# Triangle steps of three batches in a new order, and a residual that the accumulator takes over

## The chip, the cores and the metric

The kernel runs on one core of a Trainium2 chip. The metric is the device time of one execution in microseconds (us), lower being better. A core has five engines with a queue each: TensorE (PE in the profile, its weight loads PEld), VectorE (DVE), ScalarE (ACT), GpSimd (POOL), and SyncE (SP), which here issues most of the DMA transfers. Each engine works its queue off in order.

## The reference, cut to what matters

The input x is 4 batches of 64 x 64 tokens with 256 channels, all in float32. Layer 0 is self-attention over the 4096 tokens of a batch with a residual. Layer 1 is a triangle attention over the 64 x 64 grid, with 8 heads of 32 channels, followed by two layer norms and an MLP:

```python
scores = jnp.einsum('bilhd,bljhd->biljh', q, k) / np.sqrt(d_k)
att = jax.nn.softmax(scores, axis=2)
out = jnp.einsum('biljh,bilhd,bljhd->bijhd', att, v1, v2)
attn_out = out.reshape(B, N, N, E) @ Wo
h = x_in + attn_out
h = _layer_norm(h, ln_agg_g, ln_agg_b)
mlp = jax.nn.relu(h @ W1 + b1) @ W2 + b2
h = mlp + h
return _layer_norm(h, ln_out_g, ln_out_b)
```

The addition `mlp + h` is the "second residual" of this document. The triple product over att, v1 and v2 is the heavy part of layer 1: the kernel multiplies att by v2 elementwise, and then sums over l with v1 as weights on TensorE.

## The kernel before, in words

The order of all work is written out by hand (a manual schedule): the order of calls in the Python code is the order in each engine's queue. Tiles come from pools of a fixed number of buffers by tag, so a new tile waits until the last readers of the tile that had the buffer are done.

For each of the four batches, `layer0` runs the attention of layer 0 and the projections q, k, v1, v2 of layer 1, and then `run_layer1` runs 32 triangle steps: four pairs of heads (`pair`) by eight groups of eight rows i (`ig`). In the triangle stages of batches 1 to 3, the token work of the batch before (output projection, both layer norms and the MLP) is woven in, one tile of 256 tokens for every two steps. The tokens of batch 3 remain for the end; its first tile still goes with the triangle stage, and `alone` does the other 15 by themselves.

One triangle step has eight products, numbered by m. `product` multiplies a [128, 64] piece of att by v2 into a [128, 2048] tile: products of list `D_` run on VectorE (L799, tile R, three buffers, reading att from PSUM), those of list `Q_` on GpSimd (L799, tile Rp, two buffers, reading the copy attP in SBUF[...]). `npool` gives GpSimd three products in even steps and two in odd ones of batches 1 to 3, so VectorE has five and six. `accumulate` (L808) multiplies a finished product on TensorE by the selector weights wsel that hold v1, in four column tiles of 32, and sums into acc; each step has two acc tiles in PSUM, and `take` (L816) copies each by ScalarE into ao, which `store` (L823) writes to memory. Between these stand the preparations of the next step: `sums` (row sums, L731, and reciprocals, L733, on VectorE), `weights` (es, L741, eight ScalarE passes), `turn` (transposes into att on TensorE, L753, and the ScalarE copy attP, L758), and `stationary` (wsel, L777, ScalarE). In the first three pairs a quarter of the next pair's scores (`scores`, sp, L704, TensorE) and its exponentials (`take_scores`, S, L714, ScalarE) goes with every two steps.

The token tile's own steps are methods of `Tokens`: `heads` (L863, L868: output projection and residual x into PSUM tile hp), `stats_a` (bn_stats of hp on VectorE), `roots` (L893, L895: logarithm and exponential on ScalarE for the inverse root), `polish` (L902 to L910: seven small operations that refine it, on GpSimd in the stage and on VectorE in `alone`), `affine_a` (L915: normed h, ScalarE), `turn` (L933 transposes into htp, and L936: hT with the norm's gain and shift), `residue` (L945, L946: z = h times gain plus shift and b2, GpSimd), `hidden` (L956) with `rectify` (L963), `outputs` (L974: second MLP product into zp), `stats_o` (L887: z = zp + z on VectorE, then bn_stats), `affine_o` (L915), and `finish` (L982, L983: gain and shift of the last norm, GpSimd, then the output transfer). The PSUM tiles hp, htp, mp and zp share two buffers.

In the code before, `run_layer1` spreads these over two steps: in the even step heads, stats_a, outputs, stats_o and roots; in the odd step polish, affine_a, affine_o, turn, residue, finish, hidden and rectify. Each accumulation follows its product closely, and scores stand before the last accumulations of the even steps.

Of the kernel before, what the change touches and what calls it, by code (L numbers as in the profile page):

```python
# [33 lines left out]
def attention_then_triangle_kernel(  # L34
# [96 lines left out]
    def add_b2():  # L131
        b2_bc = work.tile([P, C], F32, tag="st", name="b2_bc", bufs=3)
        nc.gpsimd.dma_start(out=b2_bc, in_=b2.partition_broadcast(P))
        nc.gpsimd.tensor_tensor(lb2_bc, lb2_bc, b2_bc, ALU.add)

    lag_sb = column(lag, 2, "lag_sb")
    lab_sb = column(lab, 2, "lab_sb")
    b1_sb = column(b1, 4, "b1_sb")
# [218 lines left out]
    def layer0(b, F, safe, rest):  # L357
# [278 lines left out]
        if old:  # L636
            rest.turn(t0)
            rest.load(t0 + 1)
            rest.residue(t0)
# [12 lines left out]
        proj(last, "v2", 1, None, stage[2][:, 1, :], nc.scalar)  # L652
        return L
# [5 lines left out]
    class Layer1:  # L659
        def __init__(self, b, io, safe):  # L660
            self.b, self.io, self.safe = b, io, safe

            self.aT = dram.tile([C, 2, N // 2, N], F32, tag="aT", name="aT")
            io["a"] = self.aT
            self.S, self.v2, self.qk, self.v1, self.att, self.ao = {}, {}, {}, {}, {}, {}

# [116 lines left out]
        def begin(self, step):  # L783
            self.R, self.begun = {}, set()
            self.acc = [None, None]
            self.ao[step] = work.tile([P, 4, 8, N], F32, tag="k8", name="ao")

        def product(self, step, m):
            n, h = divmod(m, 2)
            att, attP = self.att[step]  # L790
            k = self.npool(step)
            if m >= 8 - k:
                R = work.tile([P, D, N], F32, tag="Rp", name="Rp")
                eng, src = nc.gpsimd, attP[:, m - 8 + k, :]
            else:
                R = work.tile([P, D, N], F32, tag="R", name="R", bufs=3)
                eng, src = nc.vector, att[:, n, ts(h, 64)]
            v2 = self.v2[step // NIG]
            eng.tensor_tensor(R, src.unsqueeze(1).to_broadcast([P, D, N]), v2[:, h], ALU.mult)  # L799
            self.R[m] = R  # L800

        def accumulate(self, step, m):
            n, h = divmod(m, 2)
            if self.acc[n // 2] is None:
                self.acc[n // 2] = pa("acc")
            acc, w, R = self.acc[n // 2], wsel[step % 2], self.R.pop(m)
            for c in range(4):
                nc.tensor.matmul(  # L808
                    acc[32 * c : 32 * c + 32, n % 2, :], w[:, n, c, 16 * h : 16 * h + 32],
                    R[:, ts(c, 8), :].rearrange("p d j -> p (d j)"),  # L810
                    start=n not in self.begun, stop=n in self.begun,
                )
            self.begun.add(n)

        def take(self, step, np, acc):
            nc.scalar.copy(self.ao[step][:, ts(np, 2)].rearrange("p k d j -> p k (d j)"), acc)  # L816
# [14 lines left out]
    class Tokens:  # L831
        def __init__(self):
            self.ios = []
            self.A = {}
            self.h, self.hT, self.hid, self.z, self.zp, self.hps = {}, {}, {}, {}, {}, {}
            self.mv = self.rs = None
# [48 lines left out]
        def stats_o(self, tt):  # L885
            z = self.z[tt]
            nc.vector.tensor_tensor(z, self.zp.pop(tt), z, ALU.add)  # L887
            self.stats(z, 2)
# [31 lines left out]
        def affine_a(self, tt):  # L920
            self.h[tt] = work.tile([P, 2, C], F32, tag="h", name="h", bufs=1)
            self.affine(self.h[tt], self.hps.pop(tt), 0)

        def affine_o(self, tt):
            self.affine(self.z[tt], self.z[tt], 2)


        def turn(self, tt):
            h = self.h[tt]
            tp = pb("htp").rearrange("p (c t) -> p c t", c=2)  # L930
            for cc in range(2):
                for n in range(2):
                    nc.tensor.transpose(tp[:, cc, ts(n, P)], h[:, n, ts(cc, P)], ident)  # L933
            hT = work.tile([P, 2, 256], F32, tag="hT", name="hT")
            for cc in range(2):
                nc.scalar.activation(  # L936
                    hT[:, cc, :], tp[:, cc, :], AF.Identity, bias=lab_sb[:, cc : cc + 1], scale=lag_sb[:, cc : cc + 1]
                )
            self.hT[tt] = hT


        def residue(self, tt):
            h = self.h.pop(tt)
            z = self.z[tt] = work.tile([P, 2, C], F32, tag="s4", name="z")
            nc.gpsimd.tensor_tensor(z, h, lag_bc.unsqueeze(1).to_broadcast([P, 2, C]), ALU.mult)  # L945
            nc.gpsimd.tensor_tensor(z, z, lb2_bc.unsqueeze(1).to_broadcast([P, 2, C]), ALU.add)  # L946
# [20 lines left out]
        def outputs(self, tt, n, apart=None):  # L967
            if n == 0:
                self.zp[tt] = pb("zp").rearrange("p (n c) -> p n c", n=2)
            zp = self.zp[tt]  # L970
            if apart is not None:
                zp = self.zp[tt + 1] = apart("zp").rearrange("p (n c) -> p n c", n=2)
            for fc in range(4):
                nc.tensor.matmul(  # L974
                    zp[:, n, :], self.hid[tt][:, fc, ts(n, P)], w2_sb[:, fc, :],
                    start=(fc == 0), stop=(fc == 3),
                )

# [9 lines left out]
        def alone(self, t0, t1):  # L988
# [5 lines left out]

            self.stats_a(t0 + 1)
            normed(0, 2)
            self.affine_a(t0 + 1)
            for tt in range(t0, t1 - 1):
# [6 lines left out]
                self.turn(tt + 1)  # L1005
                self.residue(tt + 1)
                if tt + 2 < t1:
                    normed(0, 2)
                    self.affine_a(tt + 2)
                for n in range(2):  # L1010
                    self.outputs(tt, n)
# [12 lines left out]
            for n in range(2):  # L1024
                V.tensor_tensor(z[:, n], self.zp[tt + n][:, n], z[:, n], ALU.add)
                self.stats(z, 2, (n,))
                normed(2 + n, 3 + n)
# [4 lines left out]


# [3 lines left out]
    def run_layer1(b, L, rest, ahead, F):  # L1037
        old = b > 0
        t0 = NP * (b - 1)

        t1 = NP * b + (b == NB - 1)
        if b == 0:
            ahead.load(0)
        waiting = behind = None
        for step in range(NSTEP):
            pair, ig = divmod(step, NIG)
            more = step + 1 < NSTEP

            now = t0 + step // 2
            nxt = now + 1  # L1050
            even, odd = old and step % 2 == 0, old and step % 2 == 1
            even_a, odd_a = even and nxt < t1, odd and nxt < t1

            forward = step // 4 * 3 + step % 4 if b == 0 and step % 4 < 3 else None
            L.begin(step)
            if F is not None:
                ahead.fetch(F, b + 1, step)
# [3 lines left out]
            L.fetch_v1(step + 2)  # L1061
            if scored:
                L.take_scores()
            if waiting is not None:
                L.take(step - 1, 1, waiting)
                L.store(step - 1)
            if step == 2:
                L.fetch_v2(1)
            if ig == 0 and 0 < pair < NPAIR - 1:
                L.fetch_v2(pair + 1)  # L1070
# [12 lines left out]
            if odd:  # L1083
                rest.polish(0 if odd_a else 2, 4, nc.gpsimd)
            if even_a:
                rest.heads(nxt, 0)
# [7 lines left out]
            if odd_a:  # L1094
                rest.affine_a(nxt)
            if odd:
                rest.affine_o(now)
            if even_a:
                rest.heads(nxt, 1)
                rest.load(nxt + 1)  # L1100
# [10 lines left out]
            if even:  # L1111
                rest.outputs(now, 0)
            L.product(step, D_[2])
            L.accumulate(step, D_[2])
            if odd_a:
                rest.turn(nxt)
# [3 lines left out]
            if even_a:  # L1120
                rest.stats_a(nxt)
            if late:
                next_weights()
            if even:
                rest.outputs(now, 1)
            if k == 3:
                L.product(step, Q_[2])
            if odd_a:
                rest.residue(nxt)
            if odd:  # L1130
                rest.finish(now)
            if odd_a:
                mps = [rest.hidden(nxt, 0), rest.hidden(nxt, 1)]
            L.product(step, D_[3])
            L.accumulate(step, D_[3])
            L.take(step, 0, L.acc[0])
# [3 lines left out]
            if odd_a:  # L1140
                rest.rectify(nxt, 0, mps[0])
                rest.rectify(nxt, 1, mps[1])
# [4 lines left out]
            if odd_a:  # L1147
                mps = [rest.hidden(nxt, 2), rest.hidden(nxt, 3)]
                rest.rectify(nxt, 2, mps[0])
                rest.rectify(nxt, 3, mps[1])  # L1150
# [9 lines left out]
            if even:  # L1160
                rest.stats_o(now)
                rest.roots(0 if even_a else 2, 4)
            if b == NB - 1 and step in (28, 29, 30):
                rest.load(t1 + step - 27, True)
            waiting = L.acc[1]
        if F is not None:
            ahead.fetch(F, b + 1, NSTEP)
        L.take(NSTEP - 1, 1, waiting)
        L.store(NSTEP - 1)

    def run(safe):
        rest, ahead = Tokens(), Ahead()
        with tc.manual_schedule():
            F = front0(0)
            for b in range(NB):
# [5 lines left out]
                run_layer1(b, L, rest, ahead, F)  # L1181
                if F is not None:
                    rest.ios.append(L.io)
            for n in range(2):
                rest.heads(NP * (NB - 1) + 1, n, psum=pc)
# [51 lines left out]
```

## Time and profile before

| what | before |
|---|---|
| time, median of 3 (range) | 3936.88 us (3935.04 to 3937.64) |
| span of the profiled execution | 3936.3 us |
| granted TensorE clock, mean | 0.994 of full speed |
| busy share PE, DVE, ACT, POOL | 95%, 69%, 46%, 49% |
| triangle stages of batches 1, 2, 3: first product to the next stage | 1373.7 to 1865.6, 2318.3 to 2811.5, 3264.1 to about 3762 us |
| lone token tiles | about 3762 to the end |

A line of a group reads: source line, engine, operation, output<-input by the program's tile names, shapes and count, then busy us in total and mean ns of one, then the engine's idle time ahead of it and what ended most of that. In a timeline a line reads: start, duration, engine, source line, operation, count of merged instructions, and in brackets the idle time of the engine ahead of it and its releaser. A matrix product in float32 appears as two instructions, so one `accumulate` (four column tiles) appears as x8. Triangle steps in pairs are called a cycle: it repeats 16 times in each stage.

### The profile page before, as it was taken

The numbers are of one execution on the slowest core, as the hardware profiler recorded it, in microseconds if no ns is written. First come the engines' busy times: TensorE is split into PE (matmuls) and PEld (weight loads), VectorE is DVE, ScalarE is ACT, GpSimd is POOL, SyncE is SP. The second block draws the span as 40 slices with busy tenths as digits, with TensorE's granted clock in tenths as the row PEclk, the third lists the DMA queues.
The fourth block names the chain that finished last, engine by engine and source line by source line (L and its number), as shares of the span: only waits on it lengthen the run. The fifth ranks groups of instructions, "written<-read, shape, count | busy, mean of one in ns | idle before, by whom it ended". The sixth has DMA issues, their size and how long they took to land.

```text
span 3936.3 us, 59354 instructions
## 1 busy us (share of the span) xinstructions
PE 3737.0 (95%) x23302; PEld 1742.6 (44%) x23302; DVE 2708.9 (69%) x2291; ACT 1814.4 (46%) x3775; POOL 1927.0 (49%) x1024
## 2 busy tenths in 40 slices
PE   9999998889999999998999999999899999999998
PEld 5444444433444444443344454444344444444376
DVE  4454499896444499998454459999644447999965
ACT  3333455554333455554333345555433335555544
POOL 4000098993000099998000049999500007999954
PEclk9999999999999999999999999999999999999999
DMA  4111445552111434323111154233211134331221
GB/s 119 50 51 48 116 139 137 136 144 96 49 51 51 121 74 91 84 53 87 52 51 46 54 131 93 55 85 74 75 48 47 49 99 103 84 85 45 53 70 50
DMA packets 439713, 309.38 MB, mean 79 GB/s; under 512 B 299328, under 2 KB 404544, under 8 KB 432128
## 3 DMA queue, kind: packets, MB, share of 16 engines
q1 hardware_dynamic: 419952, 291.12, 28.2%
q10 hardware_dynamic: 16240, 8.59, 0.8%
q0 software_dynamic: 3232, 5.78, 0.6%
q8 instruction: 186, 3.05, 0.3%
q14 instruction: 103, 0.84, 0.1%
HBM read 165.88 MB, written 139.46 MB: 78 GB/s over the span
## 4 chain that ended last, share of the span: by engine, by line
PE 72%; ACT 9%; DVE 6%; DMA 5%; POOL 3%; issue 3%; SPq 3%; ACTq 0%; POOLq 0%; DVEq 0%
PE o L432 24%; PE acc L808 12%; PE proj L489 8%; PE s L410 7%; PE mp L956 5%; PE zp L974 3%; DVE R L799 3%; PE sp L704 3%; PE v1p L514 3%; POOL Rp L799 2%; ACT S L714 2%; ACT ao L816 2%; SPq L823 2%; PE hp L863 2%; PE y L474 1%
## 5 line engine op out<-in xcount | busy, mean ns | idle before, releaser
L799 POOL TENSOR_TENSOR Rp<-attP,v 128x2048 f32<-128x2048 f32 x328 | 1490.1, 4569 | 449.9 <-DMA qk<-k 324.7
L799 DVE TENSOR_TENSOR R<-att,v 128x2048 f32<-128x2048 f32 x696 | 1547.3, 2273 | 95.4 <-PE acc L808 44.2
L439 DVE TENSOR_TENSOR esum<-esum,e 128x2048 f32<-128x2048 f32 x224 | 512.7, 2289 | 583.4 <-ACT e L421 580.5
L808 PE MATMUL acc<-R,wsel 128*32 128x512 f32 x5568 | 727.7, 605 | 64.3 <-DVE R L799 43.1
L421 ACT ACTIVATE e<-s 128x1024 f32<-128x1024 f32 x512 | 496.5, 1021 | 403.6 <-PE s L410 381.8
L902 POOL TENSOR_SCALAR nt<-mv 128x4 f32<-128x4 f32 (+1 forms) x51 | 9.9, 193 | 1283.6 <-DVE mv L880 1279.5
L816 ACT COPY ao<-acc 128x1024 f32<-128x1024 f32 x256 | 261.5, 1021 | 547.2 <-PE acc L808 436.2
L432 PE MATMUL o<-e,vlo 128*128 128x512 f32 x1024 | 473.7, 605 | 0.0
L432 PE MATMUL o<-e,vhi 128*128 128x512 f32 x1024 | 472.6, 605 | 0.0
L808 PE MATMUL acc<-Rp,wsel 128*32 128x512 f32 x2624 | 350.7, 610 | 35.1 <-POOL Rp L799 34.9
L808 PEld LDWEIGHTS acc<-R,wsel 128*32 128x32 f32 x5568 | 143.2, 109 | 396.0 <-issue 198.7
L432 PEld LDWEIGHTS o<-e,vlo 128*128 128x128 f32 x1024 | 184.0, 189 | 280.8 <-issue 280.8
L432 PEld LDWEIGHTS o<-e,vhi 128*128 128x128 f32 x1024 | 184.3, 189 | 279.7 <-issue 279.7
L410 PE MATMUL s<-gT,fT 32*128 32x512 f32 x2048 | 302.2, 640 | 4.8 <-ACT e L421 4.5
L956 PE MATMUL mp<-hT,w 128*128 128x256 f32 x1024 | 250.4, 390 | 39.6 <-ACT hT L936 39.6
L741 ACT ACTIVATE es<-S,rd 128x64 f32<-128x64 f32 x1024 | 258.4, 338 | 26.9 <-DVE rd L733 25.0
L451 DVE RECIPROCAL rec<-den 128x512 f32<-128x512 f32 x32 | 107.4, 3357 | 215.6 <-PE den L449 215.6
L974 PE MATMUL zp<-w,hid 128*128 128x256 f32 x1024 | 247.3, 387 | 2.9 <-ACT hid L963 2.9
L956 PEld LDWEIGHTS mp<-hT,w 128*128 128x128 f32 x1024 | 182.9, 189 | 117.4 <-ACT hT L936 57.8
L974 PEld LDWEIGHTS zp<-w,hid 128*128 128x128 f32 x1024 | 186.5, 191 | 67.5 <-issue 40.3
L501 ACT COPY st<-proj 128x512 f32<-128x512 f32 x104 | 60.9, 585 | 293.2 <-issue 165.9
L410 PEld LDWEIGHTS s<-gT,fT 32*128 32x128 f32 x2048 | 82.9, 182 | 193.7 <-issue 172.6
(153 smaller groups left out, 3795.3 us busy)
## 6 DMA issues: line engine op xcount, KB each, us to landing
v<-v2d SPq DMA_DIRECT2D x24, 1024.0 KB, 13.0
v1c<-v1d SPq DMA_DIRECT2D x128, 128.0 KB, 3.0
aT<-ao SPq DMA_DIRECT2D x1024, 16.0 KB, 1.9
A<-aT SPq DMA_DIRECT2D x256, 64.0 KB, 2.1
out_dram<-z SPq DMA_DIRECT2D x63, 256.0 KB, 2.2
y<-yT SPq DMA_DIRECT2D x56, 256.0 KB, 2.0
q<-st SPq DMA_DIRECT2D x56, 256.0 KB, 2.6
v1d<-st SPq DMA_DIRECT2D x56, 256.0 KB, 2.2
```

What stands on the lines that cost most here:

```text
L410: nc.tensor.matmul(s_ps[r // 2][:, r % 2, :], fT[rows, tt, ts(n, P)], gT[rows, ts(qb, QB)], start=True, stop=not safe,)
L421: nc.scalar.activation(e[g][:, 2 * j : 2 * j + 2, :], s_ps[j], AF.Exp)
L432: nc.tensor.matmul(o_ps[qb], F.v[tt][:, r * 4 + n, :], es[:, r, :], start=(k == 0 and r == 0), stop=(k == 7 and r == 3),)
L439: nc.vector.tensor_tensor(esum[qb], esum[qb], es, ALU.add)
L489: nc.tensor.matmul(ps, w[:, cc, rows], y(qb, cc), start=(cc == 0), stop=(cc == 1))
L514: nc.tensor.matmul(ps[:, ts(n, C)], y(qb, cc)[:, ts(m * 2 + n, P)], wv1_sb[:, cc, :], start=(cc == 0), stop=(cc == 1),)
L741: nc.scalar.mul(self.e[:, i, :], rows[:, i, :], rec[:, i : i + 1])
L799: eng.tensor_tensor(R, src.unsqueeze(1).to_broadcast([P, D, N]), v2[:, h], ALU.mult)
L808: nc.tensor.matmul(acc[32 * c : 32 * c + 32, n % 2, :], w[:, n, c, 16 * h : 16 * h + 32], R[:, ts(c, 8), :].rearrange("p d j -> p (d j)"), ...
L816: nc.scalar.copy(self.ao[step][:, ts(np, 2)].rearrange("p k d j -> p k (d j)"), acc)
L956: nc.tensor.matmul(self.mp[:, fc % 2, :], w1_sb[:, cc, ts(fc, P)], self.hT[tt][:, cc, :], start=(cc == 0), stop=(cc == 1),)
L974: nc.tensor.matmul(zp[:, n, :], self.hid[tt][:, fc, ts(n, P)], w2_sb[:, fc, :], start=(fc == 0), stop=(fc == 3),)
```

## The change

Three things are changed for batches 1 to 3, and the stage of batch 0 keeps the old order (`first_layer1`).

1. *New order.* `next_layer1` starts each step with the first product on GpSimd and on VectorE, and then closes the step before (its last two accumulations, the copy of its second acc, the store): the end of one step lies in the next. Accumulations stand in groups of two or three. The even step has outputs, stats_a, stats_o, roots, polish, affine_a, affine_o and turn; the odd step has hidden, rectify, finish and the heads of the tile after the next. Scores follow a table `due` and stand at the step's end. The aim is that fewer waits fall between products and accumulations.
2. *Second residual on TensorE.* `residue` and the addition in `stats_o` go for these tiles. `carried` makes a second copy of the turned h with gain, shift and b2 (hT2, ScalarE), and `outputs` adds its transposes into the accumulator zp. The statistics and `affine_o` read zp directly.
3. *Lone tiles.* h alternates between tags "h" and "A", z between "s4" and "es"; for the first tile outputs come ahead of turn; the two halves of the last tile are both summed before the first is closed. The lone tiles keep `residue`.

In `layer0`'s end the heads of the second tile are computed as well, and the next tile is loaded.

```diff
@@ Layer1, Tokens
-        def take(self, step, np, acc):
-            nc.scalar.copy(self.ao[step][:, ts(np, 2)].rearrange("p k d j -> p k (d j)"), acc)
+        def take(self, step, np):
+            nc.scalar.copy(
+                self.ao[step][:, ts(np, 2)].rearrange("p k d j -> p k (d j)"), self.acc[step][np]
+            )
...
         def stats_o(self, tt):
-            z = self.z[tt]
-            nc.vector.tensor_tensor(z, self.zp.pop(tt), z, ALU.add)
-            self.stats(z, 2)
+            z = self.z.get(tt)
+            if z is not None:
+                nc.vector.tensor_tensor(z, self.zp.pop(tt), z, ALU.add)
+            self.stats(self.zp[tt] if z is None else z, 2)
...
-        def affine_a(self, tt):
-            self.h[tt] = work.tile([P, 2, C], F32, tag="h", name="h", bufs=1)
+        def affine_a(self, tt, far=False):
+            tag = "A" if far and tt % 2 else "h"
+            self.h[tt] = work.tile([P, 2, C], F32, tag=tag, name="h", bufs=1)
...
+        def carried(self, tt):
+            self.h.pop(tt)
+            self.hT2[tt] = self.turned(lab2_sb, tag="s4")
...
                 nc.tensor.matmul(
                     zp[:, n, :], self.hid[tt][:, fc, ts(n, P)], w2_sb[:, fc, :],
-                    start=(fc == 0), stop=(fc == 3),
-                )
+                    start=(fc == 0), stop=(fc == 3 and tt not in self.hT2),
+                )
+            if tt in self.hT2:
+                for cc in range(2):
+                    nc.tensor.matmul(
+                        zp[:, n, ts(cc, P)], self.hT2[tt][:, cc, ts(n, P)], ident,
+                        start=False, stop=(cc == 1), is_transpose=True,
+                    )
...
@@ next_layer1, which takes the place of run_layer1 for batches 1 to 3
+            product(Q_[0])
+            product(D_[0])
+            if step > 0:
+                close(step - 1)
...
+            if step % 2 == 0:
+                for n in range(2):
+                    rest.outputs(now, n)
+                if more:
+                    L.stationary(step + 1)
+                if first:
+                    rest.stats_a(nxt)
+                product(D_[1])
+                if more:
+                    L.sums(step + 1)
+                    L.weights(step + 1)
+                add(D_[0], D_[1], Q_[0])
+                product(Q_[1])
+                if more:
+                    L.turn(step + 1)
+                product(D_[2])
+                add(D_[2], Q_[1])
+                rest.stats_o(now)
+                k0 = 0 if first else 2
+                rest.roots(k0, 4)
+                rest.polish(k0, 4, nc.gpsimd)
+                product(Q_[2])
+                product(D_[3])
+                if first:
+                    rest.affine_a(nxt)
+                rest.affine_o(now)
+                if first:
+                    rest.turn(nxt)
+                add(D_[3])
+                L.take(step, 0)
+                if first:
+                    rest.normed(nxt)
+                    rest.carried(nxt)
+                product(D_[4])
+                pend = [D_[4], Q_[2]]
...
+            else:
...
+                    mps = [rest.hidden(nxt, fc) for fc in range(2)]
...
+                add(D_[0], D_[1])
...
+                    mps = [rest.hidden(nxt, fc) for fc in range(2, 4)]
...
+                add(Q_[0], D_[2])
+                if more:
+                    L.turn(step + 1)
+                product(D_[3])
+                rest.finish(now)
+                add(D_[3], Q_[1])
+                L.take(step, 0)
+                product(D_[4])
...
+                        rest.heads(aft, n)
...
+            if step in due:
+                L.scores(*due[step])
+            if step % 2 == 1:
+                product(D_[5])
+                pend = [D_[4], D_[5]]
```

## The prediction

> **What bounds the kernel now.** I read the page's busy times first, then the stretches of 50 us, then the timeline and the chain of waits inside one two-step cycle, then the lone token tiles at the end. From the page (engine, busy us and share; then groups with count, busy, mean ns):
>
> ```profile
> PE 3737.0 (95%) x23302; PEld 1742.6 (44%) x23302; DVE 2708.9 (69%) x2291; ACT 1814.4 (46%) x3775; POOL 1927.0 (49%) x1024
> ...
> L799 POOL TENSOR_TENSOR Rp<-attP,v 128x2048 f32<-128x2048 f32 x328 | 1490.1, 4569 | 449.9 <-DMA qk<-k 324.7
> L799 DVE TENSOR_TENSOR R<-att,v 128x2048 f32<-128x2048 f32 x696 | 1547.3, 2273 | 95.4 <-PE acc L808 44.2
> ```
>
> The shares are averages over stages, so the busy times by stretch (PE, PEld, DVE, ACT, POOL), one inside a changed triangle stage and one in the lone tiles:
>
> ```profile
> 1550.00:1600.00 50.00, 47.16 (x367) 22.73 (x360) 46.96 (x39) 28.14 (x76) 47.99 (x25) 1.00 0.16 40
> ...
> 3850.00:3900.00 50.00, 48.40 (x234) 40.52 (x233) 31.76 (x109) 24.10 (x67) 25.36 (x20) 1.00 0.21 59
> ```
>
> In the triangle stage three engines are 94 to 96% busy: no engine can be relieved alone. What sets the cycle is in the chain of waits there (start, us, what):
>
> ```profile
> 1572.40 1.04 PE acc L808 x8
> ...
> 1573.51 1.02 ACT ao L816
> ...
> 1574.58 2.03 PE sp L704 x64
> ...
> 1576.63 2.05 ACT S L714 x2
> 1578.67 0.86 ACT ao L816
> 1579.53 1.90 ACT es L741 x8
> ...
> 1582.35 1.02 ACT h L915 x2
> ```
>
> TensorE stands still three times in it (before sp, after sp, before mp) because ScalarE's queue does the copies one after another. The cycle closes at 31.0 us: starts of the output's last pass (L983) are 31.0, 31.0, 31.0, 30.1 us apart. The durations that I use are in the timeline:
>
> ```profile
> 1567.10 0.66 PE L753 MATMUL att<-ident,es 128*128 128x128 f32 x4
> ...
> 1567.85 0.27 ACT L758 COPY attP<-att 128x128 f32<-128x128 f32 x1 [2.20 <-PE att L753]
> ...
> 1574.55 0.30 ACT L893 ACTIVATE ln<-mv,eps 128x4 f32<-128x4 f32 x1
> ...
> 1574.88 0.20 ACT L895 ACTIVATE rs<-ln 128x4 f32<-128x4 f32 x1
> ...
> 1579.39 0.20 POOL L903 TENSOR_TENSOR nt<-rs 128x4 f32<-128x4 f32 x1
> ...
> 1581.03 4.56 POOL L799 TENSOR_TENSOR Rp<-attP,v 128x2048 f32<-128x2048 f32 x1
> ```
>
> At the end, one lone tile takes 10.2 us, by this loop through POOL and an output DMA:
>
> ```profile
> 3902.91 1.27 POOL L983 TENSOR_TENSOR z<-z,lob_bc 128x512 f32<-128x512 f32 x1
> ...
> 3906.47 1.26 POOL L945 TENSOR_TENSOR z<-h,lag_bc 128x512 f32<-128x512 f32 x1 [2.30 <-DMA out_dram<-z]
> ...
> 3907.77 1.02 ACT L915 ACTIVATE h<-hp,rn 128x256 f32<-128x256 f32 x2 [4.96 <-DVE nt L902]
> 3908.39 1.00 PE L933 MATMUL htp<-ident,h 128*128 128x128 f32 x4 [1.74 <-ACT h L915]
> ```
>
> h waits until L945 has read the only h buffer, and L945 waits until z's buffer has been written out.
>
> **What the Trainium skill says.** "TensorEngine Tiling (Array Packing)", Key Properties: changing the tiling mode drains TensorE. The trace agrees: a group of accumulations takes 0.88 us inside a run and 0.97 to 1.00 where an untiled matmul follows (accumulations start at 1587.02 and 1587.91, the next matmul at 1588.88), so grouping is worth about 0.1 us for each run saved. "Perfetto Trace Analysis", Identifying the Most-Contended Engine: matmul busy time is no measure of TensorE's headroom; so I sum block starts instead. "SBUF — State Buffer", Who interferes with whom: a VectorE op with two SBUF inputs and a GpSimd op lock each other out. In the lone tiles L904 takes 1.15 us beside L983 and 0.16 without it; in the triangle stage products read PSUM and show no such thing.
>
> **The change, part by part.** A cycle is two steps; even step E has vector products D0 to D4 and POOL products Q5 to Q7, odd step O has D0 to D5 and Q6, Q7.
>
> *Work removed.* The second residual leaves POOL (L945, L946: 2 x 1.28 = 2.6 us a cycle) and VectorE (L887: 0.69). VectorE falls to 11 x 2.21 + 4 x 0.55 (bn) + 2 x 0.83 (sums) = 28.2 us a cycle, POOL to 5 x 4.55 + 1.9 (polish) + 2.6 (finish) = 27.2.
>
> *Work added.* ScalarE makes a second pair of 128x256 passes (hT2, 2 x 0.51 us, from the hT row); it is 56% busy, and they stand behind hT and ahead of the second acc copy, which waits for Q7 anyway: nothing. TensorE gets four transposes into zp, 4 x 0.11 = 0.44 (the yc transposes).
>
> *Order.* The score matmuls move to the odd step's end, behind the two heads (2.27 us), in which ScalarE copies the accumulator away: both waits around sp go. But the number of accumulation runs stays at eight a cycle, so grouping itself brings nothing. And the statistics move: stats, roots, polish and h now follow one another within one even step, and POOL's third product Q7 stands behind the polish. Queue orders of the changed kernel: ScalarE has attP ahead of Ln; POOL has polish ahead of Q7; TensorE has Q7's accumulation ahead of everything of the odd step. That is a closed loop. Its part off TensorE, from the start of att: attP starts 0.72 later (0.70 to 0.75), Ln 0.20 after it, rs 0.33 and 0.20 long, POOL 0.04 + 1.65 (1579.39 to 1581.03), product 4.55, 0.05 to TensorE: 7.74 us. TensorE's own part from Q7's accumulation to the next att: 0.97; mp 1.92; two acc 1.86; mp 1.92; two acc 1.86; att 0.59; two acc 1.86; heads 2.27; sp 1.93; two acc 1.86; zp 1.92 + 1.73 + 0.44 = 4.09; three acc 2.73; sum 23.86. Cycle 31.60 us with scores, 29.67 without. TensorE uses 4.3 of the 7.74 (D2, Q6, htp, D3, D4) and idles 3.4: first for h, then for Q7. Queued behind that wait are the hidden matmuls, and through them the whole odd step. VectorE, 28.2, and POOL, 27.2, fit inside; with three R buffers VectorE is ahead at each of its accumulations, and es is ready 0.5 us before att's turn (acc copy 1.02, S 2.05, wsel 0.99, es 2.02 after the closing accumulations).
>
> *Stage sum.* Eleven cycles have scores, then three without, then two without heads or hidden, where VectorE sets 28.4 and 27.5. With 1.45 from the first product to the cycle's origin and 1.86 to close: 1.45 + 347.6 + 89.0 + 55.9 + 1.86 = 495.8. In the first cycle the third product waits for the DMA of v2d out of a stage tile, as before (until 1383.9), and now the statistics stand behind it: 2.5 us more, 498.3. Before: 1373.7 to 1865.6 = 491.9 and 2318.3 to 2811.5 = 493.2. So +6.4 and +5.1. In batch 3 all five late cycles have heads and hidden: 1.45 + 347.6 + 148.4 + 1.86 = 499.3, and the same DMA wait ended later (3277.3): 5.6 us; 504.9 against 3264.1 to 3762.0 plus 2.3 for two heads that move in, 500.2: +4.7. Together +16.2. The hT2 passes in the end of layer 0, where TensorE waits for ScalarE at times: +1 for all.
>
> *Lone tiles.* h alternates between two buffers, z between two tags: the POOL loop goes, and TensorE's own 2.17 + 0.43 + 3.46 + 3.45 = 9.5 us is left. 14 x 0.65 = 9.1 less. Outputs ahead of the first turn save about 1.3, the earlier h in the tile before the last 1.3, closing the last two halves together about 1 (VectorE's polish of one no longer waits for the other's multiply). Together -12.7.
>
> Sum: +16.2 + 1 - 12.7 = +4.5 us: 3936.9 + 4.5, about 3941 us.
>
> **Rivals.** *Slower:* the loop has more in it than I count. If es misses its 0.5 us, or each handover costs 0.1 more (7 of them), 33 scored cycles gain 0.5 and 15 others 0.3: +21, about 3962. For it: every such error goes one way, a queue cannot be earlier than its chain. Against it: in the kernel before, the chain of 31.0 us has no unexplained gap over 0.04. *Faster, a little:* my att-to-attP or block starts are 0.3 to 0.4 us a cycle too long (a modelled end, a drain counted twice), and the lone tiles bring 15: 48 x 0.35 + 2 = -19 against the forecast, about 3922. *Faster, much:* the loop does not bind because Q7's accumulation or the roots come earlier than the queues say; then TensorE's 28.2 and VectorE's 28.2 bind, some 28.8 a cycle against 30.8: 48 x 2 + 12.7 = -109, 3828. The saturated three engines speak for it as the aim; the three queue orders speak against it.
>
> **How the numbers follow.** Forecast 0.40 (3929 to 3945, within 0.2%), slower 0.35, a little faster 0.20, much faster 0.05. Range 3912 to 3970: it leaves out the much faster case, and the ends of the two near ones.
>
> **What would show it.** Right: in the triangle stage L983 starts about 31.6 us apart and 29.7 in the last cycles; TensorE idles some 2 us before htp (released by h) and 1 us before an acc of Rp (released by POOL L799 after the polish); sp starts without a wait for ao; lone tiles 9.5 us apart. Wrong: a cycle under 30.5 with scores (the loop is not closed), one over 32.2 (a second wait, then look at es and S on ScalarE), or lone tiles still at 10.2.

## The result: slower, and the profile after

| what | before | changed |
|---|---|---|
| time, median (range) of 4 runs each | 3935.96 us (3933.39 to 3937.64) | 3980.37 us (3975.71 to 3981.99) |
| ratio to before, with its interval | | 1.0111 [1.0094, 1.0129] |
| span of the profiled execution, granted TensorE clock | 3936.3 us, 0.994 | 3973.9 us, 0.987 |

The change costs 1.1%; 3941 us was forecast. The page of the changed kernel, with engines' busy times and the two product rows (columns as before):

```profile
PE 3749.0 (94%) x23498; PEld 1782.4 (45%) x23498; DVE 2703.7 (68%) x2242; ACT 1857.9 (47%) x3873; POOL 1803.1 (45%) x928
...
L807 DVE TENSOR_TENSOR R<-att,v 128x2048 f32<-128x2048 f32 x696 | 1558.9, 2275 | 190.0 <-PE acc L817 153.0
L807 POOL TENSOR_TENSOR Rp<-attP,v 128x2048 f32<-128x2048 f32 x328 | 1487.7, 4568 | 424.0 <-ACT attP L766 386.9
```

GpSimd has lost 124 us of work (1927.0 to 1803.1), the removed residual, and the products' mean times have not moved. But VectorE's idle time ahead of its products has doubled (95.4 to 190.0), most of it until accumulations release its R buffers, and GpSimd now waits for attP. The stretches of the changed kernel (columns PE, PEld, DVE, ACT, POOL, clock, DMA) answer to the two shown before:

```profile
1550.00:1600.00 50.00, 45.43 (x364) 21.52 (x362) 44.64 (x39) 31.10 (x82) 39.80 (x25) 0.97 0.14 33
3850.00:3900.00 50.00, 47.02 (x233) 40.33 (x232) 38.39 (x115) 26.26 (x70) 23.34 (x20) 1.00 0.28 78
```

In the triangle stage no engine is saturated any more: TensorE fell from 47.16 to 45.43, VectorE from 46.96 to 44.64, GpSimd from 47.99 to 39.80. Each now waits for another, which is what a closed chain looks like. Here it is, from the chain of waits of the changed kernel (start, us, what):

```profile
1651.26 0.60 PE att L761 x4
...
1651.94 0.27 ACT attP L766
1652.20 0.21 ACT ln L905
...
1652.43 0.21 ACT rs L907
...
1654.17 0.23 POOL rn L922
1654.40 4.52 POOL Rp L807
...
1658.96 1.06 PE acc L817 x8
1660.03 1.92 PE mp L985 x8
```

From the start of att to the accumulation of Q7 it takes 7.70 us. TensorE fills part of that and waits twice; its waits from 1500 to 1700 us (us in total, times, longest):

```profile
PE htp L950 <- ACT h L927: 11.0, 6, 2.0
PE acc L817 <- POOL Rp L807: 3.8, 4, 1.0
```

For the lengths of the cycles I take the starts of the last pass of the output (L1018; before L983), in batch 1 the first eleven intervals, and then the three without scores:

| kernel | intervals, us | without scores, us |
|---|---|---|
| before | 31.9, 31.0, 31.0, 30.1, 31.1, 31.0, 31.0, 30.1, 31.1, 31.0, 31.0 | 30.1, 30.9, 30.1 |
| changed | 34.9, 31.7, 31.7, 32.2, 31.7, 31.7, 32.3, 31.7, 31.8, 32.2, 31.7 | 30.5, 29.8, 29.8 |

Where the 37.6 us between the two spans lie: the three triangle stages 11.2, 8.9 and 8.8 (503.1, 502.1 and 509.0 us against 491.9, 493.2 and 500.2, the last with the 2.3 of the two heads that moved in), batch 0's stage 6.0 (439.0 against 433.0), the stretches of layer 0 0.9 (the first) and 1.4 (the other three), and the lone tiles 0.5 (172.5 against 172.0). These sum to 37.7 by their rounded values. The profiled execution of the changed kernel is its shortest, 3975.71, and the median lies 4.7 above it.

The lone tiles should have become shorter and did not: their last passes (L1018) are mostly 10.3 us apart, those of before 10.2. Timeline of the changed kernel in one of them, GpSimd, VectorE, ScalarE and TensorE (start, duration, and so on; in brackets the idle time ahead and its releaser):

```profile
3878.80 1.27 POOL L1018 TENSOR_TENSOR z<-z,lob_bc 128x512 f32<-128x512 f32 x1
...
3878.94 1.15 DVE L916 TENSOR_TENSOR nt<-nt 128x2 f32<-128x2 f32 x1
3880.03 1.27 POOL L974 TENSOR_TENSOR z<-h,lag_bc 128x512 f32<-128x512 f32 x1
...
3880.12 1.20 DVE L917 TENSOR_SCALAR nt<-nt 128x2 f32<-128x2 f32 x1
...
3881.38 1.28 POOL L975 TENSOR_TENSOR z<-z,lb_bc 128x512 f32<-128x512 f32 x1
3881.55 1.13 DVE L921 TENSOR_TENSOR rn<-mv,rn 128x2 f32<-128x2 f32 x1
...
3885.19 1.55 ACT L992 ACTIVATE hid<-mp,b_sb 128x256 f32<-128x256 f32 x4
...
3885.70 3.72 PE L1003 MATMUL zp<-w,hid 128*128 128x256 f32 x16 [0.56 <-ACT hid L992]
```

The wait of L974 for z's output transfer is gone as forecast, so GpSimd's passes run back to back. Three of the small VectorE operations of polish stand beside them and end just after a GpSimd pass ends: 1.15, 1.20 and 1.13 us instead of 0.16 or 0.17. Statistics, roots and hid come that much later, and TensorE waits 0.56 us for hid. In the kernel before two small operations of a tile were held, too: L904 for 1.15 us beside L983, and L902 for 0.90 beside L945. Its groups of VectorE, 3800 to 3960 us (busy us, mean ns, idle before):

```profile
L904 DVE TENSOR_TENSOR nt<-nt 128x2 f32<-128x2 f32 (+1 forms) x25 | 16.0, 639 | 0.9
L902 DVE TENSOR_SCALAR nt<-mv 128x2 f32<-128x2 f32 (+1 forms) x24 | 12.4, 515 | 0.8
```

### The profile page after: what moved, and what is told of

Its sections match the earlier page's. It is cut to its first block, busy times and chain, and to the rows that moved or that the text cites. A ratio compares the mean times of both kernels' runs of the same rounds, so it can differ in the third digit from the quotient of the medians.

```text
span 3973.9 us, 59686 instructions
## 1 busy us (share of the span) xinstructions
PE 3749.0 (94%) x23498; PEld 1782.4 (45%) x23498; DVE 2703.7 (68%) x2242; ACT 1857.9 (47%) x3873; POOL 1803.1 (45%) x928
## 3 DMA queue, kind: packets, MB, share of 16 engines
q1 hardware_dynamic: 419952, 291.12, 27.8%
## 4 chain that ended last, share of the span: by engine, by line
PE 81%; POOL 8%; DVE 3%; ACT 3%; issue 2%; DMA 2%; SPq 0%; ACTq 0%; POOLq 0%; DVEq 0%
PE o L434 23%; PE acc L817 16%; PE proj L491 8%; PE s L412 7%; POOL Rp L807 6%; PE mp L985 6%; PE zp L1003 5%; PE sp L712 3%; PE v1p L516 3%; PE hp L874 3%; DVE R L807 2%; PE att L761 2%; PE y L476 1%; PE den L451 1%; DMA xin<-in_x_dram 1%
## 5 line engine op out<-in xcount | busy, mean ns | idle before, releaser
L749 ACT ACTIVATE es<-S,rd 128x64 f32<-128x64 f32 x1024 | 258.1, 337 | 31.4 <-DVE rd L741 28.9
L1003 PEld LDWEIGHTS zp<-w,hid 128*128 128x128 f32 x1024 | 186.4, 191 | 69.3 <-issue 37.7
L817 PEld LDWEIGHTS acc<-Rp,wsel 128*32 128x32 f32 x2624 | 73.7, 112 | 248.3 <-issue 131.3
```

Source lines behind the costliest of these rows:

```text
L749: nc.scalar.mul(self.e[:, i, :], rows[:, i, :], rec[:, i : i + 1])
L817: nc.tensor.matmul(acc[32 * c : 32 * c + 32, n % 2, :], w[:, n, c, 16 * h : 16 * h + 32], R[:, ts(c, 8), :].rearrange("p d j -> p (d j)"), ...
L1003: nc.tensor.matmul(zp[:, n, :], self.hid[tt][:, fc, ts(n, P)], w2_sb[:, fc, :], start=(fc == 0), stop=(fc == 3 and tt not in self.hT2),)
```

## The experiments

The questions: is the loop att, attP, roots, polish, Q7 what binds (against: too many waits of ScalarE or the four transposes); what holds the lone tiles; and is batch 0's stage really longer. Ratios are to the kernel before. Those with one run have no interval.

**1. The attP copy behind the roots.** ScalarE's queue has the roots first, so roots, polish and h no longer stand behind att in it.

```diff
...
-                    L.turn(step + 1)
+                    L.turn(step + 1, copy=False)
                 product(D_[2])
                 add(D_[2], Q_[1])
                 rest.stats_o(now)
                 k0 = 0 if first else 2
                 rest.roots(k0, 4)
+                if more:
+                    L.copied(step + 1)
                 rest.polish(k0, 4, nc.gpsimd)
```

> The changed kernel with one move: in even steps the ScalarE copy attP stands behind the roots instead of ahead of them. Theory loop (a closed chain att, attP, roots, polish, third GpSimd product, its accumulation, the odd step on TensorE sets 31.7 us a cycle): the roots no longer wait for att, start when the statistics are ready (about 2 us earlier), and the cycle falls to 29.3 to 29.8 us with scores and about 28.6 without; time 3890 to 3905 us. Rival buffers (VectorE with its three R buffers, at 28 us of work, sets the cycle): still 31 or more, time 3970 to 3985.

Measured: 3893.48 us (3892.21 to 3895.19), ratio 0.9887 [0.9870, 0.9903]. All cycles with scores after the first are 29.8, those without 27.9 to 28.0 (about 28.6 was expected). One moved copy of 0.27 us turns 1.1% slower into 1.1% faster. The waits of TensorE in this kernel, 1500 to 1700 us:

```profile
PE acc L821 <- POOL Rp L811: 5.4, 6, 0.9
```

The wait for h has gone, as it should if h was late through the roots behind attP. The chain of waits of this kernel shows what binds next (start, us, what):

```profile
1570.71 1.01 ACT ao L829
1571.72 1.91 ACT S L722 x2
...
1574.41 2.02 ACT es L749 x8
1576.43 0.20 ACT ln L909
...
1578.61 4.55 POOL Rp L811
...
1583.20 1.06 PE acc L821 x8
```

ScalarE's copy, S, wsel and es stand ahead of the logarithm, and through polish and Q7 they still hold TensorE 0.9 us a cycle.

**2. Q7 ahead of the polish on GpSimd.** The same loop, broken on the other engine: Q7 starts sooner, h comes a product later.

```diff
                 rest.roots(k0, 4)
-                rest.polish(k0, 4, nc.gpsimd)
                 product(Q_[2])
+                rest.polish(k0, 4, nc.gpsimd)
```

> The changed kernel with GpSimd's third product of an even step ahead of the polish. GpSimd stands idle some 2.6 us before the polish. Theory loop: that product must wait for its Rp buffer (the accumulation of Q5 at about 8.7 us of the cycle), ends at 13.3, and polish, h and htp come after it: cycle about 34 us with scores, 32 without, time about 4090. Rival idle (the product fills GpSimd's idle time, so Q7 is early and h as before): cycle 30.6, time about 3930.

Measured, one run: 4171.47 us; cycles, after the first of batch 1, 35.5 to 37.1 with scores, 33.9 to 34.4 without. TensorE's waits from 1500 to 1700 us in this kernel, and then its stretch (columns as before):

```profile
PE htp L950 <- ACT h L927: 32.5, 6, 5.4
```

```profile
1550.00:1600.00 50.00, 44.58 (x339) 20.64 (x341) 38.60 (x30) 26.75 (x70) 36.68 (x19) 0.91 0.19 43
```

The direction is that of the theory: htp waits 5.4 us for h, and all of the odd step stands behind it. The size is larger than expected, by 1.5 to 3.1 us a cycle with scores, by 2 without and by some 80 us in all. The clock (0.91 in the stretch, mean 0.962) accounts for most of the excess in the cycles with scores. From the start of htp to the next mp TensorE takes 4.7, 5.7 and 6.2 us in the cycles of 35.6, 36.6 and 37.0 or 37.1; the same work takes 3.5 in the short cycles of the changed kernel (4.46 less the wait of 0.95 in it). Without these 1.2, 2.2 and 2.7 us all three are about 34.4, an estimate close to the 34 expected. For the cycles without scores this was not worked out.

**3. The accumulation of Q7 later.** It and the accumulator's copy stand behind two of the hidden blocks, so that TensorE has work while Q7 runs; the turned h comes ahead of the first accumulator copy on ScalarE.

```diff
-            if step > 0:
+            if step > 0 and step % 2 == 0:
                 close(step - 1)
+            if step % 2 == 1:
+                L.accumulate(step - 1, pend[0])
+                if first:
+                    mps = [rest.hidden(nxt, fc) for fc in range(2)]
+                L.accumulate(step - 1, pend[1])
+                L.take(step - 1, 1)
+                L.store(step - 1)
...
-                L.take(step, 0)
                 if first:
                     rest.normed(nxt)
+                L.take(step, 0)
+                if first:
                     rest.carried(nxt)
...
-                    mps = [rest.hidden(nxt, fc) for fc in range(2)]
```

> The changed kernel with the accumulation of Q7, and the second copy of acc behind it, put after the first two hidden blocks on TensorE, and hT ahead of the first copy of acc on ScalarE. Theory loop: the hidden matmuls no longer stand behind GpSimd's product; only the wait for h before htp stays: cycle 29.5 to 30.0 us with scores, 28.5 to 29 without, time 3895 to 3915. Rival buffers: the wait moves to other accumulations, cycle 31 or more, time 3960 or more.

Measured: 3948.34 us (3940.66 to 3956.33, 9 runs), ratio 1.0029 [1.0019, 1.0039]; cycles 30.8 with scores, where 29.5 to 30.0 was expected, and 28.9 without, but for the first of each batch and four long ones. With scores neither theory met it, and the total missed the 3895 to 3915 expected. The time scatters by 16 us from run to run, and the granted clock goes with it: 0.990 in the two shortest runs (the shortest is the profiled one), 0.986 in the longest. Whether the longer ones have more long cycles no profile shows. TensorE's waits in this kernel, 1500 to 1700 us:

```profile
PE htp L950 <- ACT h L927: 11.0, 6, 1.9
```

The wait for Q7 has gone (0.95 us; the cycle is 0.9 shorter), and the one for h is untouched: htp is ahead of that accumulation in TensorE's queue. I had let a later accumulation shorten a wait that stands before it. The run separates the two waits: 31.7 are 1.83 for h (11.0 / 6), 0.95 for Q7, and 28.9 of TensorE's own work, which experiment 7 shows alone.

**4. The second residual alone, in the order of before.** `residue` and the addition in `stats_o` go, `carried` and the transposes come; everything else is the kernel before.

```diff
-            rest.residue(t0)
+            rest.carried(t0)
...
+            if tt in self.hT2:
+                for cc in range(2):
+                    nc.tensor.matmul(
+                        zp[:, n, ts(cc, P)], self.hT2[tt][:, cc, ts(n, P)], ident,
+                        start=False, stop=(cc == 1), is_transpose=True,
+                    )
...
+                rest.carried(nxt)
...
-            if odd_a:
-                rest.residue(nxt)
```

> The order of the kernel before with the second residual alone turned into the accumulator; no new order, lone tiles as before. Theory (the cycle of before is TensorE with ScalarE's copies, not GpSimd or VectorE): it gains the four transposes, 0.44 us, and nothing from the relief of GpSimd (2.6 us) and VectorE (0.7 us): cycle 31.2 to 31.6 with scores instead of 31.0, and 15 to 25 us more in all, about 3955. Rival (the saturated GpSimd and VectorE did set the cycle): 30.2 or less, about 3900. For batch 0's stage, which has the old code here: 433 us as before if its lengthening to 436 to 440 in the changed kernels comes from their code there.

Measured: 3947.63 us (3942.52 to 3951.34, 7 runs), ratio 1.0029 [1.0018, 1.0040]; cycles 31.3, 31.4, 31.4, 30.4 to 30.5. So in the old order the residual's move costs 0.3 to 0.4 us in nearly every cycle, about the 0.44 of the four transposes, and the relief of GpSimd brings nothing. The two extra passes of ScalarE do not add to TensorE's waiting: the waits listed for TensorE from 1500 to 1700 us are 10.4 us in all here and 10.7 before. Three of the four groups of before, which has none for a product of GpSimd:

```profile
PE mp L956 <- ACT hT L936: 5.6, 6, 1.1
PE sp L704 <- ACT ao L816: 2.2, 7, 0.3
PE acc L808 <- ACT S L714: 2.0, 6, 0.4
```

The stretch of this kernel (columns as before):

```profile
1550.00:1600.00 50.00, 46.66 (x372) 21.77 (x368) 45.41 (x33) 32.69 (x87) 44.70 (x27) 1.00 0.15 39
```

GpSimd is busy 44.70 us of 50 here instead of 47.99, and the cycle is longer. GpSimd, at 96% in the kernel before, was not what bound it. TensorE with its waits for ScalarE's copies is what is left to name; no run shortened those copies alone. The total came out below the 15 to 25 us that I expected (11).

**5. Lone tiles with the residual in the accumulator.** GpSimd has only `finish` left in these tiles; the last one keeps `residue`.

```diff
...
-                self.residue(tt)
+                if tt < t1 - 1:
+                    self.carried(tt, "es")
+                else:
+                    self.residue(tt)
```

> The changed kernel, in which the lone tiles but the last also take the second residual through the accumulator (carried in place of residue), so that GpSimd has only the two additions of finish in a tile. Theory (the freed GpSimd work locks VectorE's polish out, three long small operations a tile instead of one, and this takes what the removed buffer loop gave): fewer of the small VectorE operations take over 1 us, one a tile or none, and the tile is left with TensorE's own 9.5 us plus four transposes of 0.11: 9.9 to 10.05 us a tile instead of 10.33, about 4 us less in all, some 3976. Rival (the lone tile is bound by something else, such as ScalarE's queue, which gets 1.0 us more a tile): 10.3 us a tile or more, whatever the small operations take.

Measured, one run: 3971.20 us, tiles 10.2 us apart (10.17 in the timeline). The three small operations of polish in the groups of VectorE, 3800 to 3960 us, first in the changed kernel (count, busy us, mean ns, idle before):

```profile
L916 DVE TENSOR_TENSOR nt<-nt 128x2 f32<-128x2 f32 x30 | 17.7, 591 | 1.0
L917 DVE TENSOR_SCALAR nt<-nt 128x2 f32<-128x2 f32 x30 | 17.4, 581 | 1.0
L921 DVE TENSOR_TENSOR rn<-mv,rn 128x2 f32<-128x2 f32 x30 | 16.3, 545 | 1.0
```

Then in this kernel:

```profile
L917 DVE TENSOR_SCALAR nt<-nt 128x2 f32<-128x2 f32 (+1 forms) x30 | 5.1, 168 | 1.0
L916 DVE TENSOR_TENSOR nt<-nt 128x2 f32<-128x2 f32 (+1 forms) x31 | 5.0, 160 | 1.1
L921 DVE TENSOR_TENSOR rn<-mv,rn 128x2 f32<-128x2 f32 (+1 forms) x30 | 4.8, 161 | 1.0
```

With the residual off GpSimd none of them is long any more, and in the tiles before the last TensorE's wait for hid is gone. But the tile became only 0.16 shorter, where 0.3 to 0.4 was expected, and the whole of the lone tiles takes 172.3 us against 172.5; so the total, 9 us under the median of the changed kernel, owes next to nothing to them. TensorE is full now: its blocks are 0.57 (htp) + 1.83 + 1.73 (zp) + 0.44 (transposes) + 3.45 (mp) + 2.17 (heads) = 10.19. My floor of 9.5 was too low; without transposes it is 9.75.

**6. Batch 0's stage.** First, in the changed kernel, the fetch of v1 in its old place:

```diff
...
             scored = step % 2 == 1 and pair + 1 < NPAIR
+            L.fetch_v1(step + 2)
...
-            fetches(L, step)
+            fetches(L, step, False)
```

> The changed kernel with the old place of the v1 fetch in the stage of batch 0 (ahead of the copy and the store of acc instead of behind them in SyncE's queue). Theory queue: the first product of batch 1's stage, 7.0 us later than before (1380.7 against 1373.7), comes back to about 1374.5, because the loads behind the stores came late; time about 3973. Rival: the 7 us come from the longer end of layer 0 (two more heads, hT2), and stay.

Measured, one run: 3980.10 us, first product of batch 1 at 1378.3: missed. Then both kernels were profiled once more, unedited.

> The kernel before once more, for a second profile of batch 0's stage. Theory (the length of that stage varies from one profile to another with the arrival of its loads, whatever the code): it differs by some us from the 433.0 of the first profile, 434 to 437. Rival (the code of the changed stage makes it longer): 433.0 to 433.5 again.

> The changed kernel once more. Theory (batch 0's stage varies from profile to profile): its stage differs from the 439.0 of the first profile, 435 to 438, as in the kernels that share its code there. Rival (code): 439 again. The cycles of the later stages stay at 31.7 and 29.8, with steps of 0.5 in about every third, and the lone tiles at 10.3.

Measured: 3939.29 and 3984.31 us. The stage took 436.0 us in the second profile of before (433.0 in the first) and 437.1 in that of the changed kernel (439.0). The cycles repeat to 0.1 us in before; in the changed kernel they are 31.7 and 29.8 with steps of about 0.5 again, and its lone tiles 10.3. The difference of 6.0 is 1.1 in the second pair. The wait for the next batch's input differs from profile to profile. TensorE's waits in batch 0's stage, in the second profile of before and then in the first of the changed kernel (us in total, times, longest):

```profile
PE tp L299 <- DMA xin<-in_x_dram: 8.3, 2, 4.2
```

```profile
PE tp L301 <- DMA xin<-in_x_dram: 9.5, 2, 5.2
```

It was 6.4 in the first profile of before, and 10.3 in the second of the changed kernel. With the old code in this stage three profiles have 433.0, 435.9 (experiment 4) and 436.0; with the new code six have 436.4 to 439.6; with the new code but the old fetch order two have 436.2 and 435.5 (experiment 7). The stage goes with this wait: 433.0 us at 6.4, 435.5 at 7.6, 436.0 at 8.3, 437.1 at 10.3 and 439.6 at 11.9 (experiment 2); only the first profile of the changed kernel, 439.0 at 9.5, stands well off. And the wait goes with the fetch order: 6.4 to 8.3 in the five profiles with the old one, 9.0 to 11.9 in the six with the new one. So the fetch order does seem to lengthen the wait, by some 2 us on the average, which is not the 6.0 of the first pair; the rest moves from one execution to the next, and its cause is not settled.

**7. All repairs together.** Experiments 1, 3, 5 and the fetch order in one kernel; its diff is theirs.

> All repairs together: attP copied ahead of the roots, the last GpSimd product's accumulation and the second copy of the odd step's start behind the first two hidden blocks, the turned h ahead of the first acc copy, batch 0's fetch order as before, and the lone tiles of lone_carried. Theory (with the roots behind attP the one wait left on TensorE is 0.9 us a cycle for the last GpSimd product): cycles of 28.9 with scores and 27.9 without, about 30 us under the 3893.5 of the roots' order alone, and 4 from the lone tiles: 3855 to 3868. Rival (ScalarE's chain take, S, wsel, es, ln takes over at 29.8): cycles stay at 29.6 to 30.0 and the total at 3885 to 3895.

Measured: 3865.70 us (3864.25 to 3868.72, 5 runs), ratio 0.9823 [0.9809, 0.9836]. Cycles with scores are 28.8 to 28.9, without 27.8 to 28.0. From 1500 to 1700 us no wait of TensorE is listed, and in the stretch it is busy all the time:

```profile
1550.00:1600.00 50.00, 50.00 (x452) 25.95 (x448) 47.89 (x42) 29.98 (x83) 45.57 (x27) 1.00 0.21 51
```

This beats both kernels, by 1.8% and by 2.9%. The rival, ScalarE's chain at 29.8, is out: experiment 3's order lets TensorE work while that chain runs. In the cycles without scores TensorE waits again, and VectorE is the full engine: it is busy 74.4 us of the 75 from 1740 to 1815. The lone tiles' repair does not show in the total: they take 172.6 us here and 171.2 in experiment 1.

## Why the prediction was wrong, step by step

- *The loop: right.* 31.60 and 29.67 us were forecast, 31.7 and 29.8 measured; 7.74 off TensorE, measured 7.70. Both waits are there with about the forecast sizes (1.8 to 2.0 for h, 1.0 for Q7), and sp waits for nothing. One count in it was off: the 4.3 us that TensorE uses meanwhile leave out att's own 0.59, so it idles 2.8 and not 3.4. The cycle does not depend on that. Experiments 1 and 3 took the two waits away one at a time, and experiment 7 both: 29.8, 30.8 and 28.9.
- *What the order and the residual bring: right in direction.* Experiment 4 shows the residual's move as a cost of 0.3 to 0.4 us a cycle. Experiment 7 has the 28.8 that the prediction gave for the case in which the loop does not bind (its 28.2 for TensorE lacked the same 0.59; the 28.8 allowed for more): against 30.8 of before, the order with these repairs and the residual are worth 2 us a cycle once the loop is opened.
- *Stage sum: failed in size, +28.9 against +16.2.* The term is 347.6 us for eleven cycles at 31.60 and 89.0 for three at 29.67 (148.4 for five in batch 3): in some 40 cycles 0.1 more each, about 4.7, and ten of them a further 0.5 to 0.7, about 6; the remaining 2 lie in the stages' first and last cycles. The 0.1 lies in TensorE's own part (31.7 less 7.70 is 24.0, not 23.86), and not in seven handovers of 0.1 as the rival "slower" had it. The steps of 0.5 were in no case of the forecast: there TensorE runs at half clock for 3.41 us after its wait, see the last section. A cycle over 32.2 had been named as the sign of a second wait; the cycles of 32.2 to 32.4 have this instead. In the second pair of profiles twelve cycles are long, and the three stages are 38.5 us longer.
- *Lone tiles: failed, +0.5 against -12.7.* This is the largest single term of the error, 13.2 us. The failing step is "the POOL loop goes, and TensorE's own 2.17 + 0.43 + 3.46 + 3.45 = 9.5 us is left". The loop went, but htp to the end of zp takes 4.16 and not 3.89 (so 9.77), and the passes that no longer wait lie beside polish: 0.56 of waiting for hid (it was 0.26 in the mean before). So a tile takes 10.33 and not 9.5, and 14 of them bring about 2 us more instead of 9.1 less; by the difference, the three smaller gains at the ends brought about 1.7 of 3.6. The prediction had quoted the Trainium skill on this, "SBUF — State Buffer", Who interferes with whom (an exclusive lock between a GpSimd operation and a VectorE operation with two SBUF inputs), and had then counted it at zero. Experiment 5 shows it: without the residual's passes the three take 0.16 us each, and the wait is gone. One of the three, L917, is a TENSOR_SCALAR with one input, as is L902 of before; the same section lists `tensor_scalar` among those that can take the shared ports in a two-port mode, and here L917 was held as long as the others. No run shows which mode it ran in.
- *Batch 0's stage: no term in the sum, measured +6.0 in one pair of profiles and +1.1 in another.* The text on the change has this stage keep the old order, but its fetches of v1 had moved behind the copy and the store of the accumulator (experiment 6). A comparison of single profiles could not have told this from no change.
- *Tails of layer 0: right in size*, +1 against +1.4 (and 0.9 in the first stretch, which was not forecast). The second pair has 5.2 there, so this agreement may be luck.

The errors sum to the miss between the profiles: 12.7 in the stages, 13.2 in the lone tiles, 6.0 in batch 0's stage and 1.3 in layer 0 (2.3 against 1) make 33.2; measured 37.6 less the 4.5 forecast is 33.1. So the mechanism of the stage was right, but its sum had no term for the clock; and the lone tiles' gain hid in the forecast what the stages cost.

## What to carry to other kernels

When a short copy that releases a long operation and a short operation that releases another engine share a queue, look at which of the two has the tighter loop: here attP, 0.27 us long but released only by att, stood ahead of the roots; moving it behind them took 1.9 us off the cycle. An engine at 95% in a profile may still be only a follower; here GpSimd's relief brought nothing. Before a wait is taken from an engine, ask also beside whom its freed work will then run, and give that a cost.

## What the runs showed of the hardware

TensorE's granted clock fell to half for 3.41 us after waits of only 1.8 us. In the changed kernel ten of some 42 cycles have this (timeline of TensorE; first a long cycle, then the next):

```profile
1591.55 0.66 PE L950 MATMUL htp<-ident,h 128*128 128x128 f32 x4 [1.80 <-ACT h L927]
1592.14 3.53 PE L817 MATMUL acc<-R,wsel 128*32 128x512 f32 x16
...
1623.80 0.66 PE L950 MATMUL htp<-ident,h 128*128 128x128 f32 x4 [1.81 <-ACT h L927]
1624.38 1.92 PE L817 MATMUL acc<-R,wsel 128*32 128x512 f32 x16
```

The same 16 instructions take 3.53 us after one wait of 1.8 and 1.92 after another. The clock over the stretch 1592.31 to 1595.72 is 0.50; over 1585 to 1592.30, 1595.73 to 1600 and 1624 to 1628 it is 1.00. The cycle is only 0.5 longer: of the 1.6 lost, the 0.95 that it waits for Q7 in other cycles (no such wait stands in this one) are taken up.

It goes with how long TensorE waits in a cycle. With both waits (1.8 and 0.95) ten of some 42 cycles are long. With the 1.8 alone (experiment 3), batch 1 has one long cycle after the first, batch 2 none and batch 3 three. With the 0.9 alone (experiment 1) and with none there is no long one. With 5.4 (experiment 2) every cycle after the first of a stage has a stretch of half clock, 3.4 or 6.8 us, and the mean clock is 0.962.

The traces also show where it comes. Within an execution the stretches of half clock in the triangle stages last 3.41 us or a multiple, and they start whole multiples of 3.41 us apart (in the changed kernel at 1496.73, 1592.31, 1687.88 and 1752.73 us: 28, 28 and 19 steps). I divided the triangle stages of all eleven profiles into such steps and summed TensorE's idle time in each that ran at full clock (gaps over 0.06 us). After 4377 steps with less than 1.79 us idle the clock fell 5 times, each near the start of a stage; after 81 with 1.79 to 1.83 it fell 49 times; after 94 with more it fell 89 times. So a wait of 0.9 does not reach the edge, one of 5.4 always passes it, and the 1.8 of the changed kernel lies on it: it counts whole when it falls inside one step, as from 1589.75 to 1591.55 (step from 1588.90), and in two parts when it does not, as from 1621.99 to 1623.80 (border at 1623.03). What decides in the cases on the edge is open, and no run moved a wait within a step to try it. A cycle of 30.8 us, as in experiment 3, is close to nine steps, so its wait keeps its place on them for many cycles; that may be why its runs scatter, and was not tried either.
